# Another order of the tiles, and layer 2's weights made earlier, in a two-layer graph attention kernel

## The chip, the cores and the metric

The kernel runs on one core of a Trainium2 chip. A core has five engines with a queue each: TensorE (PE; its weight loads are shown apart as PEld), VectorE (DVE), ScalarE (ACT), GpSimd (POOL) and SyncE (SP). Each takes its instructions in order, and they wait for each other through semaphores. Transfers between main memory and the on-chip memory run on 16 DMA engines and are started from the queues of SP, ACT or POOL. The metric is the device time of one execution in microseconds (us); lower is better.

## The reference

A graph of 10000 nodes with 768 numbers each, and 170000 edges (80000 random ones in both directions, and a self-loop for each node), sorted by target; the reference adds each self-loop a second time. Two graph attention layers, the first with 4 heads of 256, the second with one head of 768, each with a norm and a residual product:

```python
def gat_conv(x, edge_index, W, a_src, a_dst, bias, heads, out_ch, concat):
    n = x.shape[0]
    ei = _add_self_loops(edge_index, n)
    src, dst = (ei[0], ei[1])
    xl = (x @ W).reshape(n, heads, out_ch)
    alpha_src = jnp.einsum('nhc,hc->nh', xl, a_src)
    alpha_dst = jnp.einsum('nhc,hc->nh', xl, a_dst)
    e = jax.nn.leaky_relu(alpha_src[src] + alpha_dst[dst], 0.2)
    m = jax.ops.segment_max(e, dst, num_segments=n)
    e = jnp.exp(e - m[dst])
    s = jax.ops.segment_sum(e, dst, num_segments=n)
    alpha = e / (s[dst] + 1e-16)
    msg = xl[src] * alpha[:, :, None]
    out = jax.ops.segment_sum(msg, dst, num_segments=n)
    out = out.reshape(n, heads * out_ch) if concat else out.mean(axis=1)
    return out + bias
...
h = relu(layer_norm(gat_conv(x, edge_index, W1, a_src1, a_dst1, b1, HEADS, HID, True), g1, be1))
h1 = h + (x @ Wr1 + br1)
h = layer_norm(gat_conv(h1, edge_index, W2, a_src2, a_dst2, b2, 1, OUT_DIM, False), g2, be2)
h = h + (h1 @ Wr2 + br2)
return _layernorm(x + h, axis=-1)
```

## The kernel before

All arithmetic is in 32-bit floating point. The work has three stages.

First (lines 578 to 644), x @ W1 is computed in 79 tiles of 128 nodes and written, with the attention terms, as rows of 1032 numbers to `table1` in main memory. Beside it the generator `prepare` (line 181) sorts the nodes by how many edges come in and lists each node's sources.

The sorted nodes are then taken in 79 tiles of 128 again. A tile has as many *slots* as its largest in-degree needs: slot k holds, for each of the 128 nodes, the number of its k-th source. `slot_counts` (line 60) fixes these counts ahead, from the size of the graph, from largest to smallest: 41, 27, 26, 25, 24, 24, 23, 23, four of 22, four of 21, six of 20, seven of 19, seven of 18, eight of 17, seven of 16, eight of 15, six of 14, five of 13, three of 12, three of 11, then 10, 9 and 8: 1377 slots. Line 93 gives each tile its place in the list of slots so that the smallest comes first, line 647 turns the counts and places round, and `nodes(t)` (line 649) and `doubled` (line 474) find the column of the t-th tile taken (`doubled` counts the second self-loop). So both layers go from 8 slots up to 41.

`Ring` (line 425) is a ring of slots on chip, 28 in layer 1 (`RING1`) and 40 in layer 2 (`RING2`). `fetch` starts a gather on POOL's queue for each slot: 128 rows of the table, chosen by the slot's node numbers. A slot can be fetched anew when all its readers are done.

Layer 1 (`ordered_layer1`, line 652): for each tile the softmax weights of the slots are made (`weights_of`), VectorE adds up the weighted rows (`weigh`, line 483, three of four slots multiplied by ACT beforehand), and TensorE takes the first two slots through diagonal matrices. Norm, residual and the product with W2 of the tile before run in between (lines 724 to 757), and `store` scatters its rows into `table2`.

Layer 2 (`ordered_layer2`, line 788) has rows of 770 numbers. Columns 0 to 511 are summed on VectorE (`weigh`, line 907) and columns 512 to 767 on TensorE (`sums`, line 826): ACT makes a diagonal matrix of a slot's weights (line 836) and TensorE multiplies the slot's rows with it into a PSUM bank `sum`. `residual` (line 840) puts x + h1 @ Wr2 of a tile into two banks. `weights_of` (line 816) makes the weights: the logits and their exponential up to its first `yield`, the division by their sum after it.

The order of the work in layer 2 is written out by hand. For a tile t it is: the diagonals and sums of t, with the norm of tile t-1 between (lines 869 to 878), then the residual of t+1, then the slots of t on VectorE (lines 904 to 915). Within this last loop, at its last three slots (`LEAD` = 3), the weights of t+1 are made, if t+1 has at most 37 slots; at slot 1 `finish` ends the norm of t-1; and each step starts one gather, 40 slots on. The scatter of tile t-1's result is issued after the loop (line 921). A tile with more slots than the ring goes through `attend_parts` (line 495): it is taken in three groups, and VectorE sums all its 768 columns. In layer 2 that is the tile of 41 slots; in layer 1 too. The vector be2 gets br1 @ Wr2 added once (`q`, lines 889 and 912).

Of the kernel before, what the change touches and what calls it, by code (L numbers as in the profile page):

```python
# [28 lines left out]
F32 = mybir.dt.float32  # L29
# [17 lines left out]
RING2 = 40  # L47
LEAD = 3
ON_PE2 = 512
# [28 lines left out]
def gnn_kernel(ctx, tc, x, x_cols, src, dst, src_col, dst_col, W1, a_src1, a_dst1, b1, g1, be1, Wr1, br1,  # L78
# [14 lines left out]
    FIRST = [sum(SLOTS[t + 1:]) for t in range(NT)]  # L93
    TOTAL = FIRST[0] + SLOTS[0]
# [379 lines left out]
    def doubled(e, t):  # L474
        nc.vector.tensor_scalar(e[:, 0], e[:, 0], loops[:, NT - 1 - t:NT - t], None, op0=OP.mult)
# [170 lines left out]

    SLOTS, FIRST = SLOTS[::-1], FIRST[::-1]

    def nodes(t):
        return order[:, NT - 1 - t:NT - t]  # L650
# [137 lines left out]
    def ordered_layer2():  # L788
        nonlocal ps_big
        with tc.tile_pool(name="b2", bufs=1) as pool, tc.tile_pool(name="small2", bufs=2) as small, \  # L790
                tc.tile_pool(name="ps_acc2", bufs=2, space=PSUM) as ps_acc, \
                tc.tile_pool(name="ps_q2", bufs=2, space=PSUM) as ps_big, tc.manual_schedule():
# [22 lines left out]
            nc.vector.memset(ones, 1.0)  # L815
            def weights_of(t):

                n = SLOTS[t]
                ad = small.tile([P, H2], F32, name="ad")
                nc.vector.tensor_add(ad, ring.slot(FIRST[t])[:, C2 + H2:], lift)  # L820
                e, _ = logits(small, ring, FIRST[t], FIRST[t] + n, ad, H2, C2)
                yield e
                normalised(small, e, H2, t)
                yield

            def sums(t, acc, e):


                n = SLOTS[t]
                nc.tensor.matmul(acc, ones, b2_b[0:1, ON_PE2:], start=True, stop=False)  # L830
                for k in range(n):
                    if k == n // 2:
                        yield
                    if k % G == 0:
                        diagonals = pool.tile([P, G, P], F32, name="diagonals", bufs=2)
                    nc.scalar.activation(diagonals[:, k % G, :], ident, AF.Copy, scale=e[:, k, :])  # L836
                    nc.tensor.matmul(acc, diagonals[:, k % G, :],  # L837
                                     ring.slot(FIRST[t] + k)[:, ON_PE2:C2], start=False, stop=(k == n - 1))

            def residual(t):  # L840
# [3 lines left out]
                for c in range(0, C2, BANK):  # L844
                    d = min(C2, c + BANK)
                    nc.tensor.matmul(r[:, c:d], ident, xt[:, c:d], start=True, stop=False)
                    for j in range(K1):
                        nc.tensor.matmul(r[:, c:d], hT[:, j, :], wr2[:, j, c:d], start=False,  # L848
                                         stop=(j == K1 - 1))
                return r  # L850

            ins = {t: fetch_x(t) for t in range(min(2, NT))}
            ring.fetch(RING2)
            rs = {}
            last = None
            ready = []
            assert SLOTS[0] <= ring.size and NT > 1
            for t in range(NT + 1):
                live, tail = t < NT, iter(())
                n = SLOTS[t] if live else 0  # L860
                whole = live and n <= ring.size
                if whole and not ready:
                    ready = list(weights_of(t))
                if whole:
                    e = ready[0]
                    acc = ps_acc.tile([P, BANK], F32, name="acc")
                    sum_ = ps_acc.tile([P, BANK], F32, name="sum")[:, :C2 - ON_PE2]
                    tail = sums(t, sum_, e)
                if last:
                    h, r, means = last  # L870
                    stats = deviation(small, [a for m in means for a in pieces(m, C2 - ON_PE2)])
                    next(tail, None)
                    scaled(h, means, stats, g2_b, be2_b)
                    nc.vector.tensor_add(h, h, r[:, :C2])
                    mean, inv = deviation(small, pieces(h, C2 // 2))
                    o = pool.tile([P, C2], F32, name="out")
                for _ in tail:
                    pass

                def finish():  # L880
                    nc.vector.reciprocal(inv, inv)
                    less = small.tile([P, 1], F32, name="less")
                    nc.vector.scalar_tensor_tensor(less, mean, -1.0, inv, op0=OP.mult, op1=OP.mult)
                    nc.scalar.activation(o, h, AF.Identity, bias=less, scale=inv)  # L884

                if live:
                    if not t:
                        rs[0] = residual(0)
                        q = product(brT, wr2, C2)
                    elif t + 1 < NT:  # L890
                        rs[t + 1] = residual(t + 1)
                    r = rs.pop(t)
                    h_ = parts[4 + t % 2][:, :C2]
                    if not whole:
                        if last:
                            finish()
                        ad = small.tile([P, H2], F32, name="ad")
                        nc.vector.tensor_add(ad, ring.slot(FIRST[t])[:, C2 + H2:], lift)
                        attend_parts(small, ring, h_, h_, ad, b2_b, H2, DH2, t)
                    ready = []  # L900
                    ahead = iter(())
# [293 lines left out]
```

## Time and profile before

| what | us |
|---|---|
| median of 3 runs (lowest, highest) | 5635.8 (5628.9, 5637.64) |
| the profiled execution's own time | 5634.25 |
| its span, first to last instruction | 5632.5 |
| first gather of layer 1 | 892.1 |
| last gather of layer 1 | 3484.7 |
| first gather of layer 2 | 3570.5 |
| last scatter of layer 2 begins | 5627.2 |

The profile is of one execution, and its times count from its first instruction. An engine's busy time leaves out what it waits and also the gaps between two instructions of a queue, so an engine can be without a pause at a good deal less than 100%. The stages have different limits, so shares of the whole span say little; the stretches between the times in the table are what to look at. "Idle before" and a name behind an arrow tell which event came last before an instruction began.

### The profile page before, as it was taken

The page shows a single profiled execution, that of the slowest core. Times are in us where ns is not written, and L with a number is a line of the kernel's source. Part 1 is how long each engine was busy: PE and PEld are TensorE (multiplying, and loading weights), DVE is VectorE, ACT ScalarE, POOL GpSimd, SP SyncE. Part 2 cuts the span into 40 slices and gives each one's busy share as a digit, 9 for nine tenths or more (in the row PEclk, how much of TensorE's full clock was granted, in tenths as well). Part 3 has the DMA queues.
Part 4 walks back from the last instruction along what each step waited for, and adds up shares of the span by engine and source line. Part 5 has one row for each costly group of instructions (what it writes and reads, how often), then busy time and mean ns, then how long its engine had stood idle before and what let it go on. Part 6 is the DMA issues. An engine that isn't in the chain of part 4 may idle for free. (4 is left out here: it accounts for less than half of the span.)

```text
span 5632.5 us, 56575 instructions
## 1 busy us (share of the span) xinstructions
PE 4694.2 (83%) x14464; PEld 2762.6 (49%) x14464; DVE 4446.0 (79%) x7881; ACT 3145.5 (56%) x8061; POOL 3411.6 (61%) x3396
## 2 busy tenths in 40 slices
PE   9999997999999998888777654499988888888772
PEld 4444444555555555444444332266556565555551
DVE  5883344788999999999998888388888887877777
ACT  3433444678878888877788766144444343333331
POOL 3446455455556666655655553477777777777773
PEclk9999998999999999999988877799999999888886
DMA  4322427789998999999998876699999999999995
GB/s 155 122 98 80 93 95 263 269 299 327 327 325 324 335 341 332 333 329 326 331 336 320 309 286 225 224 315 330 331 327 332 326 333 324 325 328 330 330 327 163
DMA packets 438659, 1580.90 MB, mean 281 GB/s; under 512 B 102764, under 2 KB 106924, under 8 KB 438327
## 3 DMA queue, kind: packets, MB, share of 16 engines
q0 software_dynamic: 341344, 1400.80, 69.9%
q1 hardware_dynamic: 93168, 170.98, 9.1%
q10 hardware_dynamic: 3814, 5.39, 0.3%
q8 instruction: 122, 2.00, 0.1%
q14 instruction: 211, 1.72, 0.1%
HBM read 1431.10 MB, written 146.19 MB: 280 GB/s over the span
## 5 line engine op out<-in xcount | busy, mean ns | idle before, releaser
L409 POOL DMA_INDIRECT ring<-table,slots x2754 | 2633.6, 956 | 1452.0 <-DVE acc L492 381.5
L492 DVE SCALAR_TENSOR_TENSOR acc<-ring,e,acc 128x256 f32<-128x256 f32 (+1 forms) x2606 | 1609.2, 618 | 134.4 <-PE acc L686 54.5
L481 ACT ACTIVATE ring<-ring,e 128x256 f32<-128x256 f32 x3536 | 1437.1, 506 | 0.0
L488 DVE TENSOR_TENSOR acc<-acc,ring 128x1024 f32<-128x1024 f32 x884 | 1089.1, 1232 | 78.6 <-DVE acc L492 0.9
L837 PE MATMUL sum<-ring,diagonals 128*128 128x256 f32 x2672 | 698.8, 425 | 258.9 <-ACT diagonals L836 256.6
L162 PE MATMUL big<-wr,xT 128*128 128x512 f32 x1896 | 867.4, 616 | 0.7 <-ACT xT L559 0.7
L848 PE MATMUL big<-w,wr 128*128 128x512 f32 (+1 forms) x2528 | 841.0, 485 | 0.0
L162 PE MATMUL big<-w,xT 128*128 128x512 f32 x1896 | 824.8, 597 | 19.1 <-DMA w<-in_W_dram 8.7
L162 PE MATMUL big<-w,hT 128*128 128x512 f32 (+1 forms) x2528 | 833.2, 487 | 1.2 <-ACT hT L559 1.2
L837 PEld LDWEIGHTS sum<-ring,diagonals 128*128 128x128 f32 x2672 | 564.8, 215 | 392.2 <-ACT diagonals L836 296.5
L162 PEld LDWEIGHTS big<-w,hT 128*128 128x128 f32 x2528 | 479.5, 190 | 375.1 <-issue 340.1
L848 PEld LDWEIGHTS big<-w,wr 128*128 128x128 f32 x2528 | 478.4, 189 | 337.0 <-issue 303.2
L162 PEld LDWEIGHTS big<-w,xT 128*128 128x128 f32 x1896 | 362.5, 192 | 478.9 <-issue 461.2
L162 PEld LDWEIGHTS big<-wr,xT 128*128 128x128 f32 x1896 | 371.6, 200 | 441.8 <-issue 440.9
L686 PE MATMUL acc<-ring,diagonals 128*128 128x256 f32 x1248 | 336.0, 430 | 277.8 <-ACT diagonals L681 245.6
L836 ACT ACTIVATE diagonals<-ident,e 128x128 f32<-128x128 f32 x1336 | 420.1, 388 | 124.2 <-PE sum L837 123.0
L884 ACT ACTIVATE out<-wr,less,sd 128x768 f32<-128x768 f32 x79 | 81.1, 1026 | 644.1 <-DMA out_dram<-out,order 556.4
L686 PEld LDWEIGHTS acc<-ring,diagonals 128*128 128x128 f32 x1248 | 269.9, 219 | 338.2 <-ACT diagonals L681 259.9
L634 DVE TENSOR_TENSOR scr<-big,as_b 128x1024 f32<-128x1024 f32 x79 | 96.7, 1225 | 382.3 <-ACT row L631 382.3
L462 ACT ACT_TABLE_LOAD x155 | 198.9, 1283 | 311.1 <-DVE e L461 283.2
L639 POOL TENSOR_TENSOR row<-row,none 128x1024 f32<-128x1024 f32 x79 | 186.9, 2366 | 270.3 <-ACT row L631 269.8
L637 ACT ACTIVATE scr<-scr 128x256 f32<-128x256 f32 x632 | 253.5, 402 | 122.9 <-DVE scr L634 122.9
(171 smaller groups left out, 3938.4 us busy)
## 6 DMA issues: line engine op xcount, KB each, us to landing
ring<-table,slots POOLq DMA_INDIRECT x2754, 5.8
table<-row SPq DMA_DIRECT2D x79, 516.0 KB, 2.9
h_d<-hT SPq DMA_DIRECT2D x79, 512.0 KB, 7.0
wr<-h_d SPq DMA_DIRECT2D x79, 512.0 KB, 6.8
xT<-in_x_cols_dram SPq DMA_DIRECT2D x79, 384.0 KB, 4.3
w<-in_W_dram SPq DMA_DIRECT2D x6, 512.0 KB, 7.3
w<-in_W_dram SPq DMA_DIRECT2D x1, 3072.0 KB, 12.9
wr<-in_Wr_dram SPq DMA_DIRECT2D x1, 3072.0 KB
```

What stands on the lines that cost most here:

```text
L162: nc.tensor.matmul(p[:, c:e], aT[:, j, :], w[:, j, c:e], start=(j == 0), stop=(j == k - 1))
L409: nc.gpsimd.indirect_dma_start(out=to, out_offset=None, in_=table, in_offset=bass.IndirectOffsetOnAxis(ap=index, axis=0), **more)
L462: nc.scalar.activation(e, e, AF.Exp)
L481: nc.scalar.activation(row[:, s], row[:, s], AF.Copy, scale=e[:, h:h + 1])
L488: nc.vector.tensor_add(acc[:, :c], acc[:, :c], row[:, :c])
L492: nc.vector.scalar_tensor_tensor(acc[:, s], row[:, s], e[:, h:h + 1], (acc if first is None else first)[:, s], op0=OP.mult, op1=OP.add)
L637: nc.scalar.activation(m[:, s], m[:, s], AF.Copy, accum_out=row[:, C1 + i * H1 + h:C1 + i * H1 + h + 1])
L639: nc.gpsimd.tensor_add(row[:, :C1], row[:, :C1], b1_b)
L686: nc.tensor.matmul(acc[:, c:d], diagonals[:, k * H1 + i, :], ring.slot(FIRST[t] + k)[:, c:d], start=(k == 0 and c % BANK == 0), stop=(k == ...
L836: nc.scalar.activation(diagonals[:, k % G, :], ident, AF.Copy, scale=e[:, k, :])
L837: nc.tensor.matmul(acc, diagonals[:, k % G, :], ring.slot(FIRST[t] + k)[:, ON_PE2:C2], start=False, stop=(k == n - 1))
L848: nc.tensor.matmul(r[:, c:d], hT[:, j, :], wr2[:, j, c:d], start=False, stop=(j == K1 - 1))
```

## The change

Three things are done.

The tiles are taken in another order, in both layers: every second tile from the smallest up, then the largest, then the others down again. The slots per tile are now 8, 10, 11, 12, 12, 13 and so on to 24, 26, 41, 27, 25, 24 and down to 12, 11, 11, 9.

```diff
-    FIRST = [sum(SLOTS[t + 1:]) for t in range(NT)]
-    TOTAL = FIRST[0] + SLOTS[0]
+    TURNS = list(range(NT - 1, -1, -2))
+    TURNS += sorted(set(range(NT)) - set(TURNS))
+    FIRST, TOTAL = [0] * NT, 0
+    for t in TURNS:
+        FIRST[t], TOTAL = TOTAL, TOTAL + SLOTS[t]
...
-    SLOTS, FIRST = SLOTS[::-1], FIRST[::-1]
+    SLOTS, FIRST = [SLOTS[t] for t in TURNS], [FIRST[t] for t in TURNS]
     def nodes(t):
-        return order[:, NT - 1 - t:NT - t]
+        return order[:, TURNS[t]:TURNS[t] + 1]
```

In layer 2 the weights of tile t+1, and with them its diagonals and TensorE's sums, are made while VectorE is in tile t: the first part at a third of tile t's slots, or at a later slot `turn` where the ring would not hold tile t+1 by then; the second part, with the sums, three slots later. The sums go into columns 768 to 1023 of the two PSUM banks of the tile's residual, which are made before, at the start of tile t; three such pairs of banks take the place of two, and the banks named `sum` are gone. There are five groups of four diagonals instead of two, and the ring of layer 2 has 38 slots instead of 40.

```diff
-RING2 = 40
+RING2 = 38
 LEAD = 3
+DIAGONALS = 5
...
             def weights_of(t):
...
                 yield e
                 normalised(small, e, H2, t)
+                to = rs[t][:, C2:2 * C2 - ON_PE2]
+                nc.tensor.matmul(to, ones, b2_b[0:1, ON_PE2:], start=False, stop=False, skip_group_check=True)
+                for k in range(n):
+                    if k % G == 0:
+                        diagonals = pool.tile([P, G, P], F32, name="diagonals", bufs=DIAGONALS)
+                    nc.scalar.activation(diagonals[:, k % G, :], ident, AF.Copy, scale=e[:, k, :])
+                    nc.tensor.matmul(to, diagonals[:, k % G, :], ring.slot(FIRST[t] + k)[:, ON_PE2:C2],
+                                     start=False, stop=(k == n - 1), skip_group_check=True)
                 yield
```

The norm of tile t-1 becomes a generator in four steps, taken at the start of tile t and ahead of its slots 3, 6 and 9; the last step issues the scatter of the result. Ahead of the tile of 41 slots all steps are taken at once. The residual of tile 0 and the product br1 @ Wr2 are issued ahead of the loop.

```diff
+            def norms(t, h, r, means):
+                stats = deviation(small, [a for m in means for a in pieces(m, C2 - ON_PE2)])
+                yield
+                scaled(h, means, stats, g2_b, be2_b)
+                nc.vector.tensor_add(h, h, r[:, :C2])
+                mean, inv = deviation(small, pieces(h, C2 // 2))
+                yield
+                nc.vector.reciprocal(inv, inv)
...
+                nc.scalar.activation(o, h, AF.Identity, bias=less, scale=inv)
+                yield
+                nc.gpsimd.indirect_dma_start(
+                    out=out, out_offset=bass.IndirectOffsetOnAxis(ap=nodes(t), axis=0),
+                    in_=o, in_offset=None, bounds_check=N - 1, oob_is_err=False)
...
-            rs = {}
+            rs = {0: residual(0)}
+            q = product(brT, wr2, C2)
...
+            for t in range(NT):
+                n = SLOTS[t]
+                if t + 1 < NT:
+                    rs[t + 1] = residual(t + 1)
+                h = parts[4 + t % 2][:, :C2]
+                if not whole(t):
+                    for _ in last:
+                        pass
...
+                    attend_parts(small, ring, h, h, ad, b2_b, H2, DH2, t)
+                    last = norms(t, h, rs[t], [h])
+                else:
+                    e = (ready or list(weights_of(t)))[0]
                     acc = ps_acc.tile([P, BANK], F32, name="acc")
...
+                    next(last, None)
+                    ready, ahead, turn = [], iter(()), n
+                    if t + 1 < NT and SLOTS[t + 1] + LEAD <= ring.size:
                         ahead = weights_of(t + 1)
-                    for k in range(n if whole else 0):
-                        if k >= n - LEAD:
+                        turn = min(max(n // 3, n + SLOTS[t + 1] + 2 * LEAD - ring.size), n - LEAD)
+                    for k in range(n):
+                        if k in (turn, turn + LEAD):
                             ready += itertools.islice(ahead, 1)
+                        if k in (LEAD, 2 * LEAD, 3 * LEAD):
+                            next(last, None)
                         weigh(acc, ring.slot(FIRST[t] + k), e[:, k], ON_PE2, None if k else b2_b)
                         ring.fetch(FIRST[t] + k + 1 + ring.size)
...
+                    ready += ahead
+                    for _ in last:
+                        pass
```

## The prediction

> **What bounds the kernel now.** I read the page's busy rows and slices first, then busy time by stage, then the gather queue's time line, the waits, and the end. The page:
>
> ```profile
> span 5632.5 us, 56575 instructions
> PE 4694.2 (83%) x14464; PEld 2762.6 (49%) x14464; DVE 4446.0 (79%) x7881; ACT 3145.5 (56%) x8061; POOL 3411.6 (61%) x3396
> PE   9999997999999998888777654499988888888772
> DMA  4322427789998999999998876699999999999995
> ```
>
> No engine is full on average. Two places are thin: slices 22 to 26, where layer 1 ends and layer 2 starts, and the last slice. Busy time by stage (columns: stretch; its length; PE, PEld, DVE, ACT, POOL busy; granted clock; DMA share; GB/s):
>
> ```profile
> 892.00:1450.00 558.00, 514.47 (x1715) 302.27 (x1716) 442.34 (x719) 404.26 (x951) 303.02 (x318) 0.98 0.86 309
> 1450.00:2900.00 1450.00, 1260.05 (x3901) 723.48 (x3900) 1334.22 (x2045) 1176.95 (x2815) 865.38 (x887) 0.94 0.92 332
> ...
> 3485.00:3570.50 85.50, 15.28 (x40) 8.59 (x40) 54.01 (x90) 36.94 (x90) 2.58 (x3) 0.58 0.17 66
> 3570.50:3700.00 129.50, 92.22 (x304) 57.87 (x304) 65.87 (x155) 30.41 (x70) 85.08 (x88) 0.84 0.85 302
> 3700.00:5460.00 1760.00, 1523.02 (x5194) 1032.29 (x5193) 1448.57 (x2966) 687.35 (x1665) 1337.89 (x1368) 0.93 0.93 328
> ...
> 5558.60:5632.50 73.90, 0.00 (x0) 0.00 (x0) 53.04 (x80) 6.25 (x11) 3.66 (x4) 0.50 0.14 40
> ```
>
> Layer 1 is TensorE's in its small tiles (514 of 558 us) and VectorE's after that (1334 of 1450). In layer 2 POOL reads only 76% busy, but its time line says more:
>
> ```profile
> 4854.21 0.94 POOL L409 DMA_INDIRECT ring<-table,slots  x1 [0.30 <-PE sum L837]
> 4855.45 0.95 POOL L409 DMA_INDIRECT ring<-table,slots  x1 [0.30 <-PE sum L837]
> 4856.70 0.95 POOL L409 DMA_INDIRECT ring<-table,slots  x1 [0.30 <-PE sum L837]
> 4857.95 0.95 POOL L409 DMA_INDIRECT ring<-table,slots  x1 [0.30 <-PE sum L837]
> ```
>
> A gather every 1.25 us: 0.95 of work and a fixed 0.30 between two, whatever is named as releaser. So 1368 DMAs in 1760 us are 1.287 us each, and POOL never rests: layer 2 is bound by the issue of its gathers. In layer 1 POOL waits for VectorE instead (waits, 1400 to 2800 us):
>
> ```profile
> POOL ring L409 <- DVE acc L492: 183.1, 149, 2.8
> POOL ring L409 <- DVE acc L488: 182.1, 372, 2.6
> ```
>
> The end: POOL's last rows.
>
> ```profile
> 5557.60 1.02 POOL L921 DMA_INDIRECT out_dram<-out,order  x1 [0.30 <-issue]
> 5570.66 1.63 POOL L409 DMA_INDIRECT ring<-table,slots  x1 [12.03 <-DVE wr L492]
> 5572.59 1.02 POOL L921 DMA_INDIRECT out_dram<-out,order  x1 [0.30 <-issue]
> 5627.15 1.00 POOL L921 DMA_INDIRECT out_dram<-out,order  x1 [53.54 <-POOLq L1143]
> ```
>
> From 5558.6 on nothing but VectorE works, on the 41-slot tile, for 73.9 us.
>
> **What the Trainium skill says.** Perfetto Trace Analysis, What "DMA-bound" means: the limit can be the sequencer that issues, its track solid with DMA slices that are descriptor generation and not transfer. The trace agrees for layer 2. SBUF — State Buffer, SBUF: two separate sides: a VectorE operation in a two-port mode keeps GpSimd from writing descriptors. That may be why some gathers take 1.15 us or more and the mean is 973 ns; the change keeps VectorE's operations, so I keep 1.287. ScalarE: Activation LUTs, What ACT_TABLE_LOAD costs: 1283 ns; the page has 1283. DMA: Bandwidth & Descriptors, Anatomy of one DMA: 2.0 us plus bytes over 436e3; for 128 rows of 3080 bytes that is an estimate of 2.9 us. The trace has 5.2, so 5.2 is used.
>
> **The change part by part.**
>
> *Order of tiles, layer 1.* The starts of line 739 on VectorE give the period of each tile size: 26.9 us up to 14 slots (TensorE), 29.7 at 16, 32.4 at 18, 36.0 at 20, 40.3 at 22, about 48 at 24, 50.5 at 25, 53.4 at 26, 44.3 at 27, 85.5 at 41. From 22 up these hold a wait, since a ring of 28 can't hold the next tile's slots early. The new order has the same sizes and again three tiles without early weights. For the tiles of 22 and more: before, 583.7. After, with the waits moved: 40.5+42.2+45.6+49.5 going up, 42.8 for 26, 85.5+7.5 for 41 (a 27 behind it now waits for its last rows, 2.5, and makes its weights late, 5), then 53+48.5+45.5+42.5+40.5+39: 582.6. The end of layer 1 (last h to the first gather of layer 2, 26.3 us) is the same chain. So layer 1: -1, between -15 and +15. The gathers' preparation has the same instructions.
>
> *Order, end of layer 2.* The last tile has 9 slots, the two ahead of it 11. When the last slot is issued VectorE is near slot 3 of the tile before the last: landing 5.2; logits 1.1; eight slots at 0.78 (row 755 ns plus a gap) 6.2; the norm of the tile before (0.75+0.48+0.15+1.02, add 0.95, statistics 1.23) 4.6; softmax division 0.9; 0.3: 18.3. Last tile: statistics 1.5, nine slots 7.0, norm 4.6, 0.3: 13.4. Last norm to the end as in the time line of before, from 5619.2: 13.3. Sum 45.0 against 73.9: -28.9.
>
> *Start of layer 2.* POOL's waits between 3570 and 3700 are 9.7+7.9 us for VectorE in six waits, 15.8 over the fixed 0.30: tile 0's end stands behind the product of br1 (22.2 us wait at L912). Now the residual and that product come first on TensorE, and the sums of tile 0 after residual 1: inputs about 3589, residual 11.6, product from 3602 to 3613, residual to 3624.5, sums from there; ring 38 is full at 3624.5. I take 5 us of POOL stalls there: -11. If TensorE starts later, up to +10.
>
> *Middle of layer 2.* Ahead of the 41-slot tile its predecessor's norm runs in one piece, with two square roots on ACT waited for; tiles of 23 to 27 make weights six slots from their end, and then a norm step of 4.6 us frees no slot. Five tiles at 2 us and 2 for the large one: +12 (0 to 30). The scatter of the result is now queued at slot 9 rather than at a tile's end; POOL is behind VectorE there, so it finds its data.
>
> *Weights early.* Removed: nothing. VectorE, ACT and TensorE have the same instructions; the sums go to the free part of the residual's banks. VectorE's waits for ACT's exponential (146.2 us at L475 from 3700 to 5460) mostly go, since three slots now lie between; ACT's for `out` go too. All were beside POOL: 0. Added: VectorE waits at a third of tile t for all of tile t+1, with the rest of tile t and its frees behind it. From 19 slots up, six slots stay free for POOL: from the issue of the last row 7 x 1.25 = 8.75 us. VectorE needs 5.2+1.1+0.8 = 7.1 to free one. It fits, by 1.6. At 17 slots nine are free. A landing of 8.0 (the longest seen) would cost 1.1; I take +4 in all (0 to 60).
>
> The landings come from this line on the ring tile, 3700 to 5460:
>
> ```profile
> DMA to landing us min/median/max: 4.1/5.2/8.0
> ```
>
> *Buffers.* Two slots fewer in the ring are in these counts. Five groups of diagonals keep ACT from waiting for TensorE (86.5 us at L836 from 4500 to 5400); hidden: 0.
>
> *Sum.* Layer 2: 1529 DMAs up to the last slot x 1.287 = 1968, +5 start, +12 middle, +4 early weights, +45 end = 2034; before 5632.5-3570.5 = 2062. So -28, with layer 1 -29: span 5603.5. The profiled execution took 5634.25, 1.8 over its span, so 5605; the median of the runs is 1.6 higher: 5606.
>
> **Rivals.**
>
> *The early wait starves the gathers (slower).* Place: VectorE at L454 in the 29 tiles with 19 slots or more. If freeing comes 3.6 us later than I have it (a landing of 8.0 and 0.8 more for the norm's step or a square root), POOL stops 2.0 us in each: 58 us, 5660. It cancels the gain from 0.95 us a tile and shows as slower from 1.35. For it: POOL has no slack at all in layer 2, so every stop is paid. Against: 1.6 us margin at the median landing.
>
> *The middle takes back what the end gives (no change).* The 41-slot tile between 26 and 27, without early weights on three tiles, stops POOL some 30 us instead of 12, and the start saves nothing: 5606+18+11 = 5635. For it: VectorE needs some 53 us for the large tile and POOL 42 x 1.287 = 54, so there is little between them.
>
> *More is won.* The 85.5 us between layer 1's last gather and layer 2's first shrink as well: small tiles leave TensorE's product waiting only 13 us. At most about 35 more: 5571. Against: the small tiles bring 26.9 us each with them, wherever they stand.
>
> That the change does not do what it says can hardly be: by the condition on the ring only the 41-slot tile and the 27-slot tile behind it go without early weights, and that is in the middle's price.
>
> **How the numbers follow.** Mine 0.60 (its own range 5588 to 5624), starved 0.13, no change 0.13, more won 0.14. What the measurement can tell is 0.2%, 11 us, so below 5624.5 is faster: 0.60 + 0.14 and a little of the second rival: 0.75. Same 0.12, slower 0.13. The range reaches from 5572 to 5640: it leaves out the starved case and some of the most favourable.
>
> **What would show it.** Right: POOL's time line in layer 2 still at 1.25 us with few longer gaps; some 45 us from the last gather to the end, with VectorE on tiles of 11 and 9; layer 1's stretch from first gather to layer 2's first unchanged at 2678 within 15. Wrong: gaps over 1 us ahead of gathers, released by VectorE at L492 or L454 in each tile of 19 slots up; fewer than 76 DMAs in 100 us of the middle; a layer 1 shorter by 20 us or more.

## The result, and the profile after

Measured one after the other on one chip, the kernel before took 5634.73 us (median of 4 runs, 5628.9 to 5637.64) and the changed one 5600.94 (4 runs, 5599.71 to 5602.47): a ratio of 0.9941, with a 95% interval from 0.9924 to 0.9959. The forecast of 5606 was 5 us high. The span of the profiled execution fell from 5632.5 to 5597.9.

That holds for chips like the first one used here. In two later sets, on two other chips, the kernel before itself took 5992 and 5945 us. On the second of these the changed kernel was the slower one; on the first it was not run. The experiments come to that.

The page of the changed kernel, the lines that answer to those shown of before (busy time, and its tenths in 40 slices of the span):

```profile
span 5597.9 us, 56699 instructions
PE 4695.8 (84%) x14464; PEld 2748.9 (49%) x14464; DVE 4424.2 (79%) x7887; ACT 3135.2 (56%) x8057; POOL 3399.5 (61%) x3396
PE   9999997999988763568888999799988747888888
DMA  4322437899999888889999996699999987999996
```

The busy times are those of before within 22 us: nothing was taken out. The thin last slice of TensorE (2) is full (8), and there are two new thin places: slices 15 to 19, layer 1's large tiles, and slice 34 with a 4 for TensorE and a 7 for the DMA engines, behind the large tile of layer 2. By stage (columns as before):

```profile
890.20:3459.60 2569.40, 2071.30 (x6512) 1204.51 (x6513) 2270.92 (x3492) 1995.50 (x4770) 1485.71 (x1530) 0.91 0.89 323
3459.60:3556.80 97.20, 83.52 (x267) 47.07 (x265) 52.86 (x85) 44.11 (x101) 4.90 (x6) 0.97 0.21 78
...
3700.00:5460.00 1760.00, 1449.19 (x4890) 968.15 (x4889) 1411.63 (x2872) 638.41 (x1576) 1313.36 (x1357) 0.90 0.92 324
...
5543.10:5597.90 54.80, 41.95 (x154) 28.11 (x152) 44.04 (x93) 17.59 (x38) 6.97 (x8) 0.92 0.21 78
```

Between the layers TensorE now works 84 of 97 us, where it had 15 of 86. After the last gather there are 54.8 us in place of 73.9, and VectorE and TensorE share them. The middle stretch holds 1357 DMAs of POOL where it held 1368: something stops the gathers there.

A sum is of use for all that follows. The span of layer 2, from its first gather to the end, is its POOL waits (what each idle time has over 0.45 us, summed up to the last gather), the DMAs times their pace without those waits, and the end after the last gather. "Layer 1" is from its first gather to layer 2's first. All in us, profiled executions of the chips where before takes 5634 to 5636:

```
                        layer 1   layer 2   POOL waits   DMAs x pace     end
before                  2678.4    2061.9      33.5       1533 x 1.2839   60.2
after                   2666.6    2041.1      39.6       1528 x 1.2740   54.8
e1 order only           2668.9    2059.9      30.0       1528 x 1.2862   64.5
e2 weights only         2681.6    2031.4      24.0       1534 x 1.2748   52.0
e3 x asked for early    2668.2    2021.6      19.0       1528 x 1.2749   54.4
e4 weights late         2669.3    2050.6      39.4       1528 x 1.2793   56.4
```

Each row is one execution. That of e1 lies 6 us under the median of e1's 20 runs, which reach over 12.6 us, and that of e2 4 us over the median of e2's; a difference of less than some 5 us between two rows carries no weight.

The 73.9 us that the prediction took for the end of before are these 60.2 and a wait of 11.7 just ahead of the last gather, with that gather itself. From before to after: layer 1 -11.8; in layer 2 waits +6.1, pace -15.1, five DMAs fewer ahead of the last gather -6.4, end -5.4.

### The profile page after: what moved, and what is told of

Same layout as the page of the kernel before. It is cut to its first block, busy times and chain, and to the rows that moved or that the text cites. A ratio compares the mean times of both kernels' runs of the same rounds, so it can differ in the third digit from the quotient of the medians.

```text
span 5597.9 us, 56699 instructions
## 1 busy us (share of the span) xinstructions
PE 4695.8 (84%) x14464; PEld 2748.9 (49%) x14464; DVE 4424.2 (79%) x7887; ACT 3135.2 (56%) x8057; POOL 3399.5 (61%) x3396
## 5 line engine op out<-in xcount | busy, mean ns | idle before, releaser
L853 PE MATMUL big<-w,wr 128*128 128x512 f32 (+1 forms) x2528 | 873.4, 499 | 0.0
L166 PE MATMUL big<-wr,xT 128*128 128x512 f32 x1896 | 852.0, 607 | 0.7 <-ACT xT L563 0.7
L166 PE MATMUL big<-w,xT 128*128 128x512 f32 x1896 | 823.0, 595 | 19.8 <-DMA w<-in_W_dram 9.2
L839 PE MATMUL big<-ring,diagonals 128*128 128x256 f32 x2672 | 658.0, 408 | 150.1 <-ACT diagonals L838 116.2
L853 PEld LDWEIGHTS big<-w,wr 128*128 128x128 f32 x2528 | 491.8, 195 | 366.9 <-issue 332.8
L839 PEld LDWEIGHTS big<-ring,diagonals 128*128 128x128 f32 x2672 | 541.4, 205 | 263.3 <-ACT diagonals L838 165.7
L690 PE MATMUL acc<-ring,diagonals 128*128 128x256 f32 x1248 | 355.0, 448 | 354.1 <-ACT diagonals L685 322.0
L690 PEld LDWEIGHTS acc<-ring,diagonals 128*128 128x128 f32 x1248 | 282.7, 230 | 421.0 <-ACT diagonals L685 337.0
L838 ACT ACTIVATE diagonals<-ident,e 128x128 f32<-128x128 f32 x1336 | 398.7, 387 | 151.2 <-DVE e L476 119.2
L542 ACT ACTIVATE sd<-mv,eps 128x1 f32<-128x1 f32 x237 | 69.8, 294 | 588.1 <-DVE mv L540 587.6
```

Source lines behind the costliest of these rows:

```text
L166: nc.tensor.matmul(p[:, c:e], aT[:, j, :], w[:, j, c:e], start=(j == 0), stop=(j == k - 1))
L690: nc.tensor.matmul(acc[:, c:d], diagonals[:, k * H1 + i, :], ring.slot(FIRST[t] + k)[:, c:d], start=(k == 0 and c % BANK == 0), stop=(k == ...
L839: nc.tensor.matmul(to, diagonals[:, k % G, :], ring.slot(FIRST[t] + k)[:, ON_PE2:C2], start=False, stop=(k == n - 1), skip_group_check=True)
```

## The experiments

In the first set, e1 to e4, the kernel before took 5636.2 us.

**e1: the order alone.** The kernel before with the change's lines for `TURNS` and nothing else.

```diff
-    FIRST = [sum(SLOTS[t + 1:]) for t in range(NT)]
+    TURNS = list(range(NT - 1, -1, -2))
+    TURNS += sorted(set(range(NT)) - set(TURNS))
...
```

> The kernel before with the new order of the tiles and nothing else; layer 2's code and its ring of 40 slots are those of before. Theory (order and early weights each win something, and in the change part of it is lost where they meet, at the 41-slot tile): layer 1 as in the changed kernel, 12 us shorter than before (2667); layer 2's gathers still at 1.287 us each, its start with about 15 us of waits of POOL, and some 50 us from its last gather to the end instead of 74; no wait of POOL over 10 us behind the 41-slot tile, since here TensorE gets a tile's sums ahead of the next tile's residual. In all 5602 to 5612. Rival (the order alone is the whole change, the early weights bring nothing): 5601 within 4 us, with the same 31 us of POOL waits behind the 41-slot tile.

Measured: 5630.51 us, ratio 0.9990 (0.9983 to 0.9997). Both expectations miss. By the medians the order alone is worth 5.7 us; in the profiles it is 9.5 us in layer 1 and 2 in layer 2. POOL's time line at its end (start, duration, idle before and who ended it):

```profile
5572.58 1.02 POOL L924 DMA_INDIRECT out_dram<-out,order  x1 [9.54 <-ACT out L887]
5589.21 1.00 POOL L924 DMA_INDIRECT out_dram<-out,order  x1 [15.62 <-ACT out L887]
5605.81 0.98 POOL L924 DMA_INDIRECT out_dram<-out,order  x1 [15.60 <-ACT out L887]
5617.10 0.98 POOL L924 DMA_INDIRECT out_dram<-out,order  x1 [10.31 <-POOLq L1146]
```

At the last gather, at 5557, VectorE was at the end of the tile of 12 slots, and the tiles of 11, 11 and 9 lay in the ring untouched. The scatters of the next two are 16.6 us apart, and the last follows 11.3 us behind. So the order trades one large tile after the last gather for three small ones: with the wait ahead of it, 71.9 us become 64.5. The wait itself, 11.7 us in before, has gone to the middle with the large tile: 12.9 us at 4596.

**e2: the weights alone.** The changed kernel, with the tiles from few slots to many as before, so the 41-slot tile is last again.

```diff
-    TURNS = list(range(NT - 1, -1, -2))
-    TURNS += sorted(set(range(NT)) - set(TURNS))
+    TURNS = list(range(NT - 1, -1, -1))
```

> The changed kernel with the tiles in the order of before, from 8 slots up to 41. Theory: layer 1 as before (2678); layer 2 starts with some 6 us of POOL waits instead of 16, its gathers come every 1.27 us instead of 1.287 (20 us over the layer), and the end after the last gather is as long as before, 60 to 74 us, since the 41-slot tile is last. No wait of POOL behind that tile, since nothing follows it. In all 5595 to 5608. Rival (early weights are beside POOL and bring nothing, as the prediction had it): gathers at 1.287, in all 5620 to 5630. Rival (early wait starves POOL): slower than 5636.

Measured: 5603.91, ratio 0.9940 (0.9923 to 0.9957): as much as the whole change. The theory has the time right and the end wrong: 52.0 us for its 60 to 74. The early weights, priced at nothing in the prediction, and what was done along with them, take 30.5 us out of layer 2: waits -9.5, pace -14.0 (one DMA more: +1.3), end -8.2. Of the waits, 8.2 us are the start (16.8 to 8.6), where the residual and br1's product now come first. POOL's end in e2:

```profile
5550.98 0.95 POOL L412 DMA_INDIRECT ring<-table,slots  x1 [0.31 <-DVE wr L495]
5552.23 1.61 POOL L412 DMA_INDIRECT ring<-table,slots  x1 [0.30 <-DVE wr L495]
5600.24 1.02 POOL L871 DMA_INDIRECT out_dram<-out,order  x1 [46.41 <-POOLq L1141]
```

The same tile of 41 slots stands there, with a smaller ring. Its last gather waits only the fixed 0.30 us, where before it waited 12.03; but three waits for TensorE's sums, 11.9 us together, have come up in the tiles ahead of it (5436 to 5515), so of this wait nothing is won, and the end's 8 us are. The largest wait of VectorE in before, 3700 to 5460 us, shows one thing that had held it back (columns: total, times, longest):

```profile
DVE e L475 <- ACT e L462: 146.2, 57, 5.6
```

In the changed kernel 1.5 us are left of it. In its place VectorE waits for gathers to land, which is what an engine ahead of POOL does:

```profile
DVE e L458 <- DMA ring<-table,slots: 178.9, 45, 9.1
```

**e3: the x rows asked for ahead of the large tile.** `fetch_x(t + 2)` of the 41-slot tile is put ahead of `attend_parts`, which starts a gather after each of its 41 slots, for the slot 38 further on.

```diff
                     for _ in last:
                         pass
+                    if t + 2 < NT:
+                        ins[t + 2] = fetch_x(t + 2)
                     ad = small.tile([P, H2], F32, name="ad")
```

> The changed kernel, with the gather of x for two tiles on issued ahead of the 41-slot tile's gathers instead of behind them. Theory (POOL's 27 us of waits behind the 41-slot tile are a chain: x of tile 41 stands in POOL's queue behind 41 ring gathers, TensorE's residual waits for it, the sums of tile 40 wait behind the residual, the diagonals on ACT behind the sums, and VectorE waits for ACT's square root): both waits of POOL (19.8 and 6.9 us) and VectorE's wait of 28.6 us go, 20 to 27 us less, 5574 to 5581. Rival (the wait is the 27-slot tile's weights, made late for want of ring slots): VectorE's wait for its slots, 8.2 us, stays and POOL still waits 20 us or more there; 5596 to 5602.

Why: POOL's time line in the changed kernel, behind the large tile:

```profile
4615.84 0.95 POOL L413 DMA_INDIRECT ring<-table,slots  x1 [0.30 <-issue]
4617.09 0.95 POOL L413 DMA_INDIRECT wr<-in_x_dram,order  x1 [0.30 <-issue]
4637.80 0.94 POOL L413 DMA_INDIRECT ring<-table,slots  x1 [19.77 <-PE big L839]
```

TensorE's in the same stretch:

```profile
4621.80 2.04 PE L850 MATMUL big<-wr,ident 128*128 128x512 f32 x2 [63.18 <-DMA wr<-in_x_dram,order]
4623.63 8.76 PE L853 MATMUL big<-w,wr 128*128 128x512 f32 x16
...
4636.83 11.92 PE L839 MATMUL big<-ring,diagonals 128*128 128x256 f32 x54
```

And what VectorE waited for between 4590 and 4700:

```profile
DVE sd L553 <- ACT sd L542: 30.2, 2, 28.6
```

Read together: the x rows of a later tile are asked for behind the 41 gathers that go out during the large tile; TensorE, in its order, stands 63 us at the residual that needs them, with the sums of the next tile behind it; ACT has no free diagonals until those sums run, so its square root is late; VectorE waits 28.6 us for the root, no slot comes free, and POOL stands 19.8. In e3 the x gather has moved up:

```profile
4560.45 1.76 POOL L413 DMA_INDIRECT wr<-in_x_dram,order  x1 [0.30 <-issue]
4562.51 0.94 POOL L413 DMA_INDIRECT ring<-table,slots  x1 [0.30 <-DVE wr L496]
```

Measured: 5585.20, ratio 0.9909 (0.9893 to 0.9926), 16 us below the changed kernel. Layer 2 is 19.5 us shorter, and its waits are 20.6 us less. The longest wait left there is 3.8, and VectorE's longest for a root is 5.3. The median is 4 us over the theory's range. But the long waits, VectorE's among them, went with the one step that was moved, so the theory's chain is their cause, and the rival falls.

The order alone doesn't make this chain. In e1 the x rows are asked for at 4655.95, behind the large tile too, and POOL stands nowhere behind it: there TensorE makes the sums of the next tile at 4649.09, ahead of the residual, which begins at 4663.22. It takes both parts of the change, the large tile in the middle and the residual put first.

**e4: the weights late.** All as changed, but the weights of tile t+1 begin three slots from tile t's end, as before.

```diff
-                        turn = min(max(n // 3, n + SLOTS[t + 1] + 2 * LEAD - ring.size), n - LEAD)
+                        turn = n - LEAD
```

> The changed kernel with the first part of the next tile's weights three slots ahead of the end of a tile, as before the change, and the second part with the sums after its last slot. Theory (layer 2 is bound by the issue of gathers, and what counts is that sums and norm no longer stand in each other's way, not how early they come): gathers stay at 1.27 us, the whole within 8 us of the changed kernel, 5593 to 5609. Rival (the earliness is what shortens the gathers' pace): back to 1.287, 5616 to 5630.

Measured: 5611.58, ratio 0.9956 (0.9939 to 0.9972), between the two expectations. Making them early is thus worth 9.5 us in layer 2, 8.1 of it pace (5.3 ns a DMA); the medians differ by 10.6. What e4 keeps of the new form (residual first, norm in steps, sums in the residual's banks, five groups of diagonals) was not taken apart further. VectorE's waits in e4, 3700 to 5460:

```profile
DVE sd L553 <- ACT sd L542: 197.2, 65, 28.7
```

In the changed kernel this line reads 38.6 in 10 times. Late weights put a tile's diagonals on ACT just ahead of the norm's square root.

**The second set, on another chip.** Here the kernel before took 5991.8 us (10 runs, 5985.3 to 6003.5), so the times named in the next four expectations, which reckon with a chip like the first, can't be read against these runs; ratios to before in the set are what is left.

e5: e3, and where a tile's weights were not made ahead (tile 0 and the one behind the large tile), its weights and sums are issued ahead of the next residual.

```diff
                 n = SLOTS[t]
+                if whole(t) and not ready:
+                    ready = list(weights_of(t))
                 if t + 1 < NT:
                     rs[t + 1] = residual(t + 1)
...
```

> As e3_x_early, and where a tile's weights were not made ahead (tile 0 and the 27-slot tile behind the 41-slot one), its weights and sums are issued ahead of the next tile's residual instead of behind it. Theory (what is left of POOL's long waits in layer 2, 5.5 us at its start and some 8 us around the 41-slot tile, are slots held by sums that stand behind a residual on TensorE): the wait at the start falls under 2 us, the others to about 4, 5575 to 5581. Rival (the order on TensorE only moves the wait to VectorE, which needs the residual and the product of br1): 5582 to 5588.

Measured 5975.78, ratio 0.9966 (0.9952 to 0.9979). What it is worth against e3 had to be asked again (f3).

e6: e3, with TensorE writing the bias into the tile's accumulator, so that VectorE's first weighing of a tile reads one operand from SBUF and one from PSUM, like the others.

```diff
+                accs[t] = ps_acc.tile([P, BANK], F32, name="acc")
+                nc.tensor.matmul(accs[t], ones, b2_b[0:1, :ON_PE2], start=True, stop=True)
...
-                        weigh(acc, ring.slot(FIRST[t] + k), e[:, k], ON_PE2, None if k else b2_b)
+                        weigh(acc, ring.slot(FIRST[t] + k), e[:, k], ON_PE2)
```

> As e3_x_early, but the bias of the first 512 columns is put into the accumulator by TensorE (a matmul of ones with the bias), so that a tile's first step on VectorE reads the accumulator in PSUM like the others and no longer two operands in SBUF. Theory (a gather that begins while VectorE runs an operation with two operands in SBUF takes longer, 1.1 to 1.3 us instead of 0.95): the 34 gathers that began under that step, 1.12 us on average in e3_x_early, take 0.95; 5.7 us less, 5577 to 5583, with the lengthening under the norm's step left as it is. Rival (the length of a gather has another cause, or shifts to another step): POOL's mean stays within 3 ns of 969 and the time is that of e3_x_early, 5582 to 5588.

Measured 6086.19, ratio 1.0158 (1.0140 to 1.0176). As a gain it failed: layer 2 is 119 us longer than in e5 on the same chip, 105 of it POOL's waits. That the added work of TensorE is what is paid for, on a chip where TensorE pauses as shown below, is a guess. For the gathers it is of use, and the last section comes back to it.

e7: e2, with the scatter of a tile's result after its last slot and not at slot 9.

```diff
-                        if k in (LEAD, 2 * LEAD, 3 * LEAD):
+                        if k in (LEAD, 2 * LEAD):
```

> As e2_weights_only, but the norm's last step, the scatter of the result, comes behind a tile's last slot, as before the change, instead of ahead of its slot 9. Theory (part of what the rewritten layer 2 wins is that the buffer of the result is free again in time; ACT's queue stood up to 19 us for it): ACT waits for the scatter again in the tiles from 19 slots up, and ahead of the 41-slot tile VectorE waits for ACT; the end is longer by some 12 to 20 us, in all 5612 to 5626. Rival (the place of the scatter costs nothing): 5600 to 5608.

Measured 6012.38, ratio 1.0031 (1.0018 to 1.0044). ACT does wait for the scatters again, 245.7 us between 3570 and 5460 us where it is 39.4 in e5 on this chip, but e2 didn't run here, so whether the scatter's place costs anything stays open.

e8: the changed kernel with two groups of diagonals.

```diff
-DIAGONALS = 5
+DIAGONALS = 2
```

> The changed kernel with two groups of four diagonals instead of five; the ring stays at 38 slots. Theory (ACT has time to spare, its waits for TensorE are hidden, as the prediction had it): within 5 us of the changed kernel, 5596 to 5606. Rival (with 8 diagonals ACT stands behind TensorE's sums, and the square roots of the norm behind ACT hold VectorE and so the ring): 5608 to 5630.

Measured 6452.59, ratio 1.0772 (1.0755 to 1.0789), far over what either expectation allows as a ratio; f4 asks again.

**The third set, to have one measure for these.** The changed kernel, e3, e5 and e8 again, together. It ran on a third chip, slower like the second: before took 5945.46 us (41 runs, 5929.9 to 5959.5).

> The changed kernel itself, once more, beside the kernel before on whatever chip this set runs on, as the measure for the three kernels that follow. In the set with e5 to e8 the kernel before took 5991.8 us where it had taken 5636.2, and the profiles of that set show TensorE in layer 2 with 1.4 to 2.4 us between matmuls that wait for nothing the profile names (some 100 of them among the residual products alone, none in the profiles of the earlier set). Theory: that is the chip and not the kernels; the order of the kernels among one another stays, so the ratio to before is near 0.994 on a chip like the first (5595 to 5606 us) and between 0.985 and 1.01 on one like the second. Rival: where TensorE is held back, layer 2 is TensorE's, and early weights, which put more of its work behind one another, make the changed kernel slower than before: ratio above 1.01 on a chip like the second.

Measured 5974.83, ratio 1.0051 (1.0033 to 1.0069). On this chip the change makes the kernel slower by half a per cent. This is within the theory's bounds, and the rival's 1.01 isn't reached; but the theory's sentence that the order of the kernels stays holds only among the changed ones. TensorE's time line in f1, in the middle of a residual:

```profile
4306.43 1.67 PE L853 MATMUL big<-w,wr 128*128 128x256 f32 x7
4308.38 0.38 PE L853 MATMUL big<-w,wr 128*128 128x256 f32 x1 [0.28 <-issue]
4309.78 0.47 PE L853 MATMUL big<-w,wr 128*128 128x256 f32 x1 [1.03 <-issue]
4311.87 0.56 PE L853 MATMUL big<-w,wr 128*128 128x256 f32 x1 [1.62 <-issue]
4313.27 0.59 PE L853 MATMUL big<-w,wr 128*128 128x256 f32 x1 [0.84 <-issue]
4316.07 0.59 PE L853 MATMUL big<-w,wr 128*128 128x256 f32 x1 [2.21 <-issue]
```

Seven matmuls start 0.22 us apart; then starts follow at 1.40, 2.09, 1.40, 2.80: multiples of 0.70 us, and the profile names nothing that is waited for. All 16 matmuls of this part of the product are in the record, so the gaps aren't missing ones. The clock recorded over that stretch, beside the one before it (PE busy, PEld, DVE, ACT, POOL, clock, DMA share, GB/s):

```profile
4299.00:4307.50 8.50, 8.50 (x24) 4.35 (x23) 3.13 (x6) 1.28 (x4) 6.51 (x7) 1.00 0.89 317
4308.00:4319.60 11.60, 3.28 (x8) 1.53 (x7) 5.43 (x10) 2.56 (x5) 6.29 (x7) 0.67 0.83 292
```

This clock doesn't tell the cause, for it is also low where TensorE merely has nothing to do: 0.50 in the last 73.9 us of before, without a single matmul.

To count such stretches: pauses of over 0.25 us between two matmuls of one line, for which the profile names nothing waited for, are joined where less than 0.7 us lie between them, and what comes to over 3 us is kept. Layer 2 of f1 has 54, 366 us together; the six profiles of the first chip, before and after among them, have none. The gathers stop too: POOL's waits in layer 2 are 387.8 us against 39.6, and that is 348 of the 365 us by which f1's layer 2 is longer than the changed kernel's on the first chip. Layer 1 is only 18.7 us longer. There is no trace of the kernel before on these chips, so that it loses less there because less hangs on TensorE at a tile's end is a guess, not shown.

> The kernel of e3 once more on the same chip: x gather of the tile two ahead asked for before the 41 gathers of the large tile. Theory: 15 to 22 us below f1, ratio to before 0.990 to 0.992 on a chip like the first; on one like the second at most 10 us below f1, since there POOL waits some 3 us in nearly every tile and a wait of 20 us in one place is made up. Rival: e3's gain over the changed kernel belonged to its one set; then less than 6 us on any chip.

Measured 5963.01, ratio 1.0024 (1.0014 to 1.0035), 11.8 us below f1 by the medians. The gain of e3 is there on another chip too, by the medians 2 us over what the theory allowed, and POOL's waits in the 100 us behind the large tile fall from 36.4 to 21.3. But the 20 runs of f2 spread from 5937.4 to 5975.5, so the size of the gain, and with it the rival's limit of 6 us, isn't settled closely.

> The kernel of e5 once more: f2 with the large tile's follower making its weights, and so its sums, ahead of the next residual. Theory: it takes away only the two or three waits of 1.3 to 2.6 us that f2 has behind the large tile: between 0 and 6 us below f2 on any chip. Rival: the residual that now stands behind those sums comes late to the norm two tiles on: 5 to 15 us above f2.

Measured 5951.17, ratio 1.0013 (1.0004 to 1.0022), another 11.8 us below f2 by the medians, where the theory has at most 6, and away from the rival. The theory left out that the edit moves tile 0 as well: POOL's waits in the first 130 us of layer 2 fall from 23.0 to 15.9, while those in the 100 us behind the large tile stay (21.3 and 20.0). On a chip like the first it didn't run.

> The changed kernel with two groups of diagonals in place of five; the prediction put the five at nothing. On the second chip it took 1.077 of before. Theory: with two groups ACT can be only eight slots ahead of TensorE, and the sums of a tile stand behind a residual of some 11 us, so ACT stops in every tile of more than eight slots and what is queued behind it (the square root, the exponential of the next tile) comes late to VectorE: slower than f1 by 60 to 250 us on a chip like the first, and by some 400 on one like the second. Rival (the prediction): ACT's wait is hidden on a chip where TensorE isn't held back: within 12 us of f1.

Measured 6438.67, ratio 1.0824 (1.0789 to 1.0859), 464 us over f1, near the 400 expected here. TensorE's line and, under it, ACT's in one tile of f4:

```profile
4304.91 3.72 PE L839 MATMUL big<-ring,diagonals 128*128 128x256 f32 x16
4321.96 7.04 PE L839 MATMUL big<-ring,diagonals 128*128 128x256 f32 x20 [13.33 <-issue]
```

```profile
4301.72 2.44 ACT L838 ACTIVATE diagonals<-ident,e 128x128 f32<-128x128 f32 x8 [2.20 <-DVE total L473]
4321.51 1.28 ACT L838 ACTIVATE diagonals<-ident,e 128x128 f32<-128x128 f32 x4 [17.34 <-remote]
```

ACT makes eight diagonals and waits 17 us for TensorE to be done with four; only then the other ten, and the square root behind them. VectorE waits 770 us for roots in this kernel between 3700 and 5800 us, where it waits 155 in f1. But ACT is released only at 4321.51, some 15 us after the first eight of TensorE's 16 matmuls, which read the four diagonals, had started; before has two groups as well, and there ACT waits at most 2.9 us for TensorE's sums between 3700 and 5460. So the pauses of TensorE on this chip seem to be part of this number. On the first chip two groups with the new form weren't tried, and whether five were needed there stays open.

## Why the prediction was right, and where its steps were wrong

The bound and the direction were foreseen; that the total came within 5 us was luck. Layer 1 gave 11 us more than reckoned, and layer 2 gave 7 less (2041 for 2034), and inside layer 2 larger errors offset each other: the DMAs took 1947 us for 1968, the waits 40 for 21, the end 55 for 45.

*The bound.* Right. POOL's gathers bind layer 2 in after as in before, at 1.25 us where nothing stops them, and every long wait that was taken away (e3) came off the time. That POOL "never rests" is a little too strong: 33.5 us in before are waits.

*Layer 1, -1 from the order: measured -12.* The tiles of 22 slots and more were foreseen at 582.6 and took 579.5, against 583.7 in before; that is 4 of the 12 us. The step that failed is that the end of layer 1 "is the same chain". From the last h, where the prediction starts to count, it is longer, 30.2 us for 26.3, because that h now lies ready for 8 us until TensorE comes to it. From the store before the last it is shorter. The stores of the last four tiles of layer 1, on POOL:

```profile
3480.87 1.01 POOL L710 DMA_INDIRECT table<-row,order  x1 [20.00 <-ACT row L708]
3507.73 0.99 POOL L710 DMA_INDIRECT table<-row,order  x1 [25.85 <-ACT row L708]
3534.58 0.97 POOL L710 DMA_INDIRECT table<-row,order  x1 [25.87 <-ACT row L708]
3548.43 0.97 POOL L710 DMA_INDIRECT table<-row,order  x1 [12.88 <-ACT row L708]
```

26.9 us apart, as the prediction had it for small tiles wherever they stand, but the last one 13.9. Before's last two stores are 20.6 apart, and that is 7 of the 12 us:

```profile
3541.41 1.01 POOL L706 DMA_INDIRECT table<-row,order  x1 [55.82 <-ACT row L704]
3561.98 0.99 POOL L706 DMA_INDIRECT table<-row,order  x1 [19.56 <-ACT row L704]
```

Between them TensorE, in before, waits for VectorE's last tile and multiplies it with W2:

```profile
3544.38 1.94 PE L556 MATMUL big<-ident,h 128*128 128x128 f32 x8 [61.15 <-DVE h L739]
3547.49 13.33 PE L162 MATMUL big<-w,hT 128*128 128x512 f32 x32 [1.16 <-ACT hT L559]
```

In the changed kernel nothing waits for VectorE there, and the same product took 10.61 us with a recorded clock of 1.00, where after the wait of 61 us it took 13.33 with 0.74. In e1 these stores are 13.9 apart too, and layer 1 is 9.5 us shorter, so the gain is the order's. The rival "more is won" had looked at this place. But the stretch that it wanted shorter is longer (97.2 us for 85.5), and the end brings 7 of its 35.

*Start of layer 2, -11: right.* POOL's waits in the first 130 us are 7.4 us against 16.8: -9.4.

*Order, end of layer 2, -28.9: measured -19.* The step put VectorE "near slot 3 of the tile before the last" when the last gather is issued, so that 45.0 us would be left. It was at slot 3 of the tile before that one, a whole tile farther back. (In the 73.9 us of before, in which the prediction has "nothing but VectorE" at work, ScalarE works 6.25 us.) The time line of VectorE, where it makes the last tile's logits:

```profile
5557.43 0.15 DVE L829 TENSOR_TENSOR ad<-ring,lift 128x1 f32<-128x1 f32 x1
5557.62 0.17 DVE L458 TENSOR_TENSOR e<-ring,ad 128x9 f32<-128x9 f32 x1
```

The last gather of that tile began at 5542.2; with the 5.2 us that a landing takes it was there some ten us before its logits. A landing had been taken for what sets VectorE's pace, where its own work in tiles of 11 slots does, about 16 us each. Nor is it all the order's: wait and end together, 71.9 us in before, are 64.5 with the order alone, 63.9 with the weights alone (52.0 and the 11.9 of waits ahead), and 54.8 with both.

*Middle, +12: measured 31.* The waits around the large tile are 3.9, 19.5, 6.6 and 1.3 us. Two square roots on ACT had been reckoned, and the right engine waits for one; but what is late is the x gather, at the other end of a chain over TensorE and ACT. The prediction has no term for it. `fetch_x` was not moved at all: its place behind `attend_parts` cost nothing while the large tile came last, the new order put 39 tiles behind it, and the residual put ahead of the sums made those tiles wait (in e1, without that, nothing does).

*Weights early, "all were beside POOL: 0", and +4: the step that was most wrong.* Without the start, which had its own term, e2 has -22 here: pace -14, end -8. The reasoning was that POOL binds, so that what VectorE saves is covered. At the end POOL has nothing more to do and covers nothing; and POOL's own pace was taken for a constant. The +4 didn't come: from 3700 on, the changed kernel has three waits of POOL of more than 0.6 us over the fixed 0.30 that aren't around the large tile, the longest 0.7. So the rival that the early wait starves the gathers fell.

*Pace, 1.287 kept: measured 1.284 before and 1.274 after.* Ten nanoseconds on 1528 DMAs are 15 us. The mean duration of these DMAs on POOL fell by as much, from 978.3 to 968.3 ns. The Trainium skill was read here (SBUF — State Buffer, SBUF: two separate sides) as concerning which operations VectorE runs, and these stayed; which gathers begin under them did not, and the last section shows what that is worth.

*Buffers, "hidden: 0".* Not settled: two groups in place of five cost 464 us on the third chip, and on the first this wasn't run.

*No change, by the middle taking back the end.* Half true: the middle did take 31 us. The rest of its sum fell, since the start, the pace, layer 1 and the end brought what they did.

## What to carry to other kernels

When the order of uneven pieces is changed, look for steps whose place was harmless only because of the old order: a load issued behind the largest piece is free while that piece is last, and can stop four engines in turn when the piece is in the middle and work that frees buffers stands behind the load. An engine that is busy but not the bound still decides the ends, where the bound resource has nothing more to do, so a saving "beside" the bound is to be priced at the start, at the end and around the largest piece before it is called nothing. Half a per cent gained on one chip can be lost on another, as here, so a gain of that size is best measured on several.

## What the runs showed that was not expected

**On two of three chips TensorE pauses in layer 2.** In the six profiles there of f1 to f3 and e5 to e7 the count above gives 46 to 58 stretches, 303 to 396 us together; on the first chip none. What sets it off isn't known from these runs, nor whether it belongs to the chips or to their state at that time, since each was used for one set: layer 1 of f1 has none, though TensorE is busy there for 489 of the first 560 us.

**A gather that begins under a VectorE operation with two operands from SBUF takes longer.** An example in before, POOL and then VectorE:

```profile
4319.47 0.95 POOL L409 DMA_INDIRECT ring<-table,slots  x1 [0.30 <-PE sum L837]
4320.72 1.22 POOL L409 DMA_INDIRECT ring<-table,slots  x1 [0.30 <-DVE mv L536]
```

```profile
4320.42 0.71 DVE L492 SCALAR_TENSOR_TENSOR acc<-ring,e,b 128x512 f32<-128x512 f32 x1
4321.16 0.76 DVE L492 SCALAR_TENSOR_TENSOR acc<-ring,e,acc 128x512 f32<-128x512 f32 x1
```

Over layer 2 of before, the 70 gathers that began under `acc<-ring,e,b` took 1241 ns on average and the 41 under `wr<-wr,sd,be` 1287, against about 948 under all others: 35 us in all. In after it is 43 at 1149, 50 at 1058 and 25 under `wr<-ring,e,wr` at 1306: 23 us. The difference is 12 of the 15 us of the pace. Nor is it the length of the operation: in before, 19 gathers began under `wr<-wr,big`, 0.95 us long with one operand in PSUM, and took 945. Over the six profiles of the first chip this extra time follows the pace:

```
                          before   e1     e4     after   e3     e2
extra time of gathers, us  35.2   40.0   29.7   23.1   23.0   21.3
pace, us a DMA            1.2839 1.2862 1.2793 1.2740 1.2749 1.2748
```

In e6, where the first weighing reads PSUM in place of the second SBUF operand, the 553 gathers under `acc<-ring,e,acc`, the first weighings among them, took 950; but the 58 under `wr<-wr,sd,be` then took 1274, so that the sum was 28.5 us, with 23.5 in e5 on the same chip, and nothing was saved. The theory is borne out for the first weighing, and the rival in that the length turned up in another step; POOL's mean over layer 2 is 972 ns. Why more gathers fell under that step isn't known. The page of the skill named above has it that such an operation locks GpSimd out only if that one reads SBUF, which would fit a gather that reads its slot numbers there; the profile doesn't show what the gather was doing at that time.
